# A recurrence's input products in four 64x64 tiles, with the side work listed by half steps

## The chip, the cores and the metric

The kernel runs on one core of a Trainium2 chip. Its metric is the time of one execution in device microseconds (us), from the first to the last instruction. The time before the change is the median of three runs. A profile of a single execution gives the rows that are read here.

The engines are called as the profile calls them: PE is the matrix engine (PEld is its weight load, which overlaps PE), ACT the scalar engine, DVE the vector engine, POOL the general-purpose engine, SP the queue that issues most transfers.

## The reference, cut to what matters

The whole is two transformer layers over 16 sequences of 512 tokens with 256 channels. The first layer (attention with latent heads, then a feed-forward part with weights and activations rounded to four bits) is not touched. The second layer begins with a recurrence over the 512 time steps, and only that part of the program changes:

```python
def _L1_attn_ref(tokens, norm_w, a, b, c, skip, w_out, b_out):
    B, T, DIM = tokens.shape
    H, D, S = b.shape                      # 16 heads, 16 channels each, 64 states each
    ms = jnp.mean(jnp.square(tokens), axis=-1, keepdims=True)
    x = tokens * jax.lax.rsqrt(ms + EPS) * norm_w
    x = x.reshape(B, T, H, D)
    a_t = jnp.tanh(a)
    state0 = jnp.zeros((B, H, S), dtype=tokens.dtype)

    def step(state, x_t):
        state = jnp.tanh(jnp.einsum('bhs,hst->bht', state, a_t) + jnp.einsum('bhd,hds->bhs', x_t, b))
        mixed = jnp.einsum('bhs,hsd->bhd', state, c) + skip[None] * x_t
        return (state, mixed)
    ...
    return tokens + outs @ w_out.T + b_out
```

After it come a layer norm, and a part without recurrence in time except that each token is mixed with the one before it: two products and a gate, then a third product, and a last layer norm.

A step's state depends on the state before it, so the 512 steps are a chain. The second term in the tanh, `x_t` times `b`, does not depend on the state: it is the input part of the title, and it can be computed for many steps at once.

## The kernel before

**Two groups.** The 16 heads are two groups `g` of 8, and a group's state of one step is a tile of 128 partitions (rows) by 64 columns. `advance_state(g, t)` (L1063) makes one step of one group: four matmuls (L1076) of state times `a`, added in PSUM to the input part that already stands there in the tile `u`, then two tanh instructions on ACT (L1084), which write the new state into `hist`. Each matmul of 32-bit floats is two instructions on PE, so the four are 8 PE instructions. The two groups alternate: while ACT works on one, PE works on the other. What stands between two calls of `advance_state` is called a half step below.

**Input part.** `inputs(u, g, t0, n)` (L1028) fills the tile `u` for up to 8 steps of one group. The weights `wb` have all 128 input rows and 64 columns, so two matmuls fit beside each other in the array (the profile writes 128*64 for that). For each step `u` has 64 columns, of which a half of the partitions uses one half of them, and the other half the other: 32 of 64 columns stay without an input part. A tile takes 16 matmuls with 64 columns each, cut into four pieces of four matmuls. `make_inputs(t)` (L1167) issues the pieces that are due at step `t`, right after the first group's step. In 16 steps that is 16 pieces.

**Side work.** All else of the second layer is worked on for blocks of 16 steps, some blocks ahead of or behind the recurrence, as generators that issue one piece at each call: N normalizes a block's tokens and turns them (two pieces, the second with four transposes on PE, L895, into the ring `xt`), R reads the states out (two pieces, L1052), A is the product with `w_out` (four, L916), M mixes neighbouring tokens (one, four transposes at L895), K and G are the products of key and gate (four each, L916), V is the last product (four, L916). The list `PERIOD` gives their order within 16 steps. At each step `left` says how many of the list's entries may be left over, so that the 21 entries are spread evenly: after the first group's step come the input piece and, where two entries fall on one step, the first of them; after the second group's step comes one entry. D is what is left of the first layer's feed-forward part of the last sequence (three times seven pieces); they stand in `LATER`, two thirds in the first 16 steps and one third in the next.

**Order.** PE's order is written out by hand: the matmuls stand in its queue in the order in which the Python code issues them. DVE, ACT and POOL are put in order by the scheduling layer, which places an instruction where it expects it to be ready. All engines work their queue strictly in order.

**States taken out.** After every 8 steps, four copies on POOL of one kind (L1208), four of another (L1212) and four copies on DVE (L1215) put the states from `hist` into the tile `clean`, in the layout that R reads. R of a block needs all copies of that block.

**Buffers.** PSUM has 8 banks: three tiles `u` of two banks each, and two banks for the results of all side work (`mm`, pool `ps_2`). A product that stays open from its first to its last piece holds one of these two banks until DVE or ACT has read it.

Of the kernel before, what the change touches and what calls it, by code (L numbers as in the profile page):

```python
# [59 lines left out]
def tile_kernel(ctx: ExitStack, tc: tile.TileContext, I: dict, out: bass.AP):  # L60
# [794 lines left out]
    def in_ring(g, t0):  # L855

        at = (t0 - g * 4) % RING
        cut = min(TS, RING - at)
        return [(0, at, cut)] + ([(cut, 0, TS - cut)] if cut < TS else [])
# [168 lines left out]
    def inputs(u, g, t0, n):  # L1028

        for k in range(2):  # L1030
            for par in range(2):
                at = (t0 - g * 4) % RING + par
                for half in range(2):
                    for r in range(2):
                        rs, bs = slice(r * 64, r * 64 + 64), half * 32 + r * 16
                        nc.tensor.matmul(  # L1036
                            u[rs, k, par:n:2, bs : bs + 16],
                            wb[:, g * 2 + k, par, half, rs], xt[:, g, at : at + n - par : 2, :],
                            start=par == 0 and half == 0, stop=False, skip_group_check=True,
                        )  # L1040
                yield
# [25 lines left out]
    def advance_state(g, t):  # L1067
        t0, _, u = us[g]
        if state[g] is not None:

            for k in range(2):
                own = state[g][:, k, :].rearrange("p (r s b) -> p r s b", r=2, s=2)
                into = u[:, k, t - t0, :].rearrange("p (s r b) -> p s r b", s=2, r=2)
                for c in range(2):
                    cs = slice(c * 64, c * 64 + 64)
                    nc.tensor.matmul(  # L1076
                        into[cs, :, c, :], ta[:, t % 2, g * 2 + k, cs], own[:, :, c, :],
# [3 lines left out]
        with tc.high_priority():  # L1081
            for r in range(2):
                rs = slice(r * 64, r * 64 + 64)
                nc.scalar.activation(  # L1084
                    state[g][rs, :, r * 32 : r * 32 + 32].rearrange("p k (s b) -> p k s b", s=2),
                    u[rs, :, t - t0, :]
                    .rearrange("p k (s r b) -> p k s r b", s=2, r=2)[:, :, :, r, :],
                    AF.Tanh,
                )

    def beside(M):

        todo = [("N", 1)] * 2 if M == 0 else []
        for e in PERIOD:
            i = M + int(e[1:])
            if 0 <= i < T // TS:
                todo.append((e[0], i))
        return todo + LATER.get(M, [])

    PERIOD = [
        "N2", "V-3", "V-3", "V-3", "V-3", "K-2", "K-2", "R-1", "R-1", "K-2", "K-2", "A-1", "A-1",
        "A-1", "A-1", "G-2", "G-2", "G-2", "G-2", "N2", "M-1",
    ]

# [5 lines left out]
    LATER = {  # L1112
        0: [
            *[("D", 1)] * 7, *[("D", 2)] * 7,
        ],
        1: [
            *[("D", 3)] * 7,
        ],
    }
# [3 lines left out]
        "U": lambda j: ffn_up(B - 1, j), "D": lambda j: ffn_down(B - 1, j),  # L1123
        "E": lambda j: iter([quantize_now(j) or 0.0]), "F": lambda j: iter([vector_done(("h", B - 1, j)) or 0.0]),
# [12 lines left out]
    with tc.manual_schedule(engines={mybir.EngineType.PE}):  # L1137
# [40 lines left out]
        for t in range(T):  # L1178
# [7 lines left out]
            if t == 0:  # L1186
                make_inputs(-1)
# [127 lines left out]
```

## Time and profile before

| what | us |
|---|---|
| median of three runs (2538.06 to 2540.24) | 2539.11 |
| span of the profiled execution | 2543.7 |
| in it: first layer, up to the first input product | 0 to 1814.0 |
| blocks 0 to 2 of 16 steps (first tanh of each: 1816.1, 1843.4, 1867.7) | 1816.1 to 1887.4 |
| blocks 3 to 30 | 1887.4 to 2491.6 |
| block 31, up to the last tanh | 2491.6 to 2514 |
| side work that is left after the last step | 2514 to 2543.7 |

Busy time over the whole span, from the first part of the page: PE 2412.0 us (95%), DVE 1925.8 us (76%), ACT 1621.3 us (64%), POOL 1035.4 us (41%). A busy share of PE is not PE at its peak, since matmuls are pipelined; what a step costs is read from the distance between the starts of instructions in the timeline.

The starts of the blocks are counted from the tanh instructions (L1084): 64 of them are one block of 16 steps of two groups. Blocks 3 to 30 take 604.25 us together, 21.58 us each on the mean, 1.35 us for a step. Block 0 takes 27.33 us, block 1 24.30, block 2 19.65 and block 31 20.12 us up to the start of what would be the next.

### The profile page before, as it was taken

How to read it: one execution, taken by the hardware profiler on the slowest of the kernel's cores; microseconds unless marked ns; L12 is line 12 of the kernel's file. 1: busy time of each engine (PE TensorE's matmuls, PEld its weight loads, DVE VectorE, ACT ScalarE, POOL GpSimd, SP SyncE). 2: the span in 40 equal slices, each digit the busy share in tenths (PEclk: the TensorE clock that was granted, in tenths of full speed). 3: DMA queues.
4: the chain of work that ended last, by engine and by line, in shares of the span. 5: the costliest groups of instructions: out<-in, count | busy, mean ns of one | idle time of the engine just before them, and what ended most of it. 6: DMA issues, size and time to landing. Idle time of an engine off the chain costs nothing.

```text
span 2543.7 us, 73791 instructions
## 1 busy us (share of the span) xinstructions
PE 2412.0 (95%) x28802; PEld 1712.7 (67%) x28802; DVE 1925.8 (76%) x5492; ACT 1621.3 (64%) x5536; POOL 1035.4 (41%) x1642
## 2 busy tenths in 40 slices
PE   7789999999999999999999999998799999999998
PEld 4455666666666666666666666655678888888885
DVE  4867888788888888888888888867756666666666
ACT  4656676676766666666666666654366666666664
POOL 4322333333333333333333333332445555555554
PEclk8889999999999999999999999989899999999999
DMA  3000000000000000000000000000111111111100
GB/s 117 24 9 6 12 24 14 16 16 12 24 14 16 16 12 24 14 16 16 12 24 14 16 14 6 16 14 9 43 32 39 37 40 41 40 38 39 36 28 27
DMA packets 58015, 61.30 MB, mean 24 GB/s; under 512 B 7873, under 2 KB 53058, under 8 KB 57666
## 3 DMA queue, kind: packets, MB, share of 16 engines
q1 hardware_dynamic: 56802, 55.54, 7.0%
q8 instruction: 226, 3.70, 0.6%
q14 instruction: 123, 1.01, 0.1%
q10 hardware_dynamic: 864, 1.05, 0.1%
HBM read 39.79 MB, written 16.78 MB: 22 GB/s over the span
## 4 chain that ended last, share of the span: by engine, by line
PE 51%; DVE 29%; ACT 10%; POOL 5%; issue 3%; DMA 1%; ACTq 0%; DVEq 0%; POOLq 0%; SPq 0%
PE u L1076 8%; DVE p L546 5%; PE ps_pt L569 5%; PE u L1036 5%; ACT p L559 4%; PE S L534 3%; PE ps_d L164 3%; DVE q_q L210 3%; ACT pT L571 3%; PE pg L164 3%; PE pu L164 2%; PE ps_h L449 2%; DVE q_sc L205 2%; DVE q_q L218 2%; PE ps_a L916 2%
## 5 line engine op out<-in xcount | busy, mean ns | idle before, releaser
L559 ACT ACTIVATE p<-p,nm 128x512 f32<-128x512 f32 (+3 forms) x1024 | 570.4, 562 | 492.3 <-DVE nm L546 488.3
L1084 ACT ACTIVATE hist<-u 64x64 f32<-64x64 f32 x2048 | 447.1, 218 | 237.4 <-PE u L1076 151.4
L546 DVE CUSTOM_DVE_ANT_0 p<-S,mask 128x512 f32<-128x512 f32 (+3 forms) x1024 | 442.9, 484 | 50.9 <-PE S L534 50.4
L1076 PEld LDWEIGHTS u<-hist,ta 128*64 128x64 f32 x8176 | 367.7, 138 | 119.9 <-ACT hist L1084 41.5
L569 PEld LDWEIGHTS ps_pt<-ident,p 128*128 128x128 f32 x2560 | 302.0, 142 | 217.3 <-issue 107.1
L571 ACT COPY pT<-ps_pt 128x384 f32<-128x384 f32 (+1 forms) x768 | 374.2, 517 | 62.3 <-PE ps_pt L569 62.1
L569 PE MATMUL ps_pt<-ident,p 128*128 128x128 f32 x2560 | 396.3, 280 | 4.5 <-DVE nm L546 3.0
L1076 PE MATMUL u<-hist,ta 128*64 128x32 f32 x8176 | 394.4, 218 | 4.6 <-ACT hist L1084 4.5
L219 POOL TENSOR_TENSOR q_q<-q_q,q_m 128x704 f32<-128x704 f32 (+1 forms) x140 | 164.1, 1172 | 372.2 <-DVE q_q L218 361.5
L534 PE MATMUL S<-kc,qr 32*128 32x512 f32 (+3 forms) x2048 | 224.1, 475 | 10.5 <-ACT qr L488 7.9
L1036 PE MATMUL u<-xt,wb 128*64 128x64 f32 x4128 | 224.9, 231 | 5.1 <-issue 5.0
L559 ACT ACTIVATION_READ_ACCUMULATOR p<-p,nm 128x1 f32 x1024 | 199.8, 195 | 0.0
L164 PE MATMUL ps_d<-wdT,hT 128*128 128x256 f32 x732 | 173.1, 386 | 13.9 <-DVE nm L546 12.1
L164 PE MATMUL pg<-wgT,xqT 128*128 128x352 f32 x512 | 177.9, 471 | 6.5 <-DVE nm L546 5.1
L483 POOL TENSOR_TENSOR qc<-qc,qs 128x512 f32<-128x512 f32 x64 | 81.5, 1273 | 235.5 <-DVE qs L482 221.1
L164 PE MATMUL pu<-wuT,xqT 128*128 128x352 f32 x512 | 173.7, 462 | 1.0 <-DVE nm L546 1.0
L1036 PEld LDWEIGHTS u<-xt,wb 128*64 128x64 f32 x4128 | 166.7, 140 | 10.3 <-issue 5.5
L600 PEld LDWEIGHTS py<-pT,vpad 128*32 128x32 f32 x5120 | 138.7, 110 | 47.0 <-issue 30.3
L600 PE MATMUL py<-pT,vpad 128*32 128x128 f32 x5120 | 162.6, 274 | 7.8 <-ACT pT L571 7.5
L164 PEld LDWEIGHTS ps_d<-wdT,hT 128*128 128x128 f32 x732 | 135.4, 192 | 37.6 <-DVE nm L546 15.4
L86 POOL TENSOR_SCALAR ve<-mv 128x2 f32<-128x2 f32 (+1 forms) x160 | 31.1, 194 | 312.4 <-DVE mv L94 309.7
L585 POOL COPY rcx<-rc 128x256 f32<-128x256 f32 x64 | 40.3, 630 | 286.9 <-DVE rc L583 260.9
(167 smaller groups left out, 4648.8 us busy)
## 6 DMA issues: line engine op xcount, KB each, us to landing
xT<-in_xT_dram SPq DMA_DIRECT2D x16, 512.0 KB
x<-in_x_dram SPq DMA_DIRECT2D x16, 512.0 KB
xs<-x SPq DMA_DIRECT2D x64, 128.0 KB
x<-xs SPq DMA_DIRECT2D x32, 256.0 KB
xm<-xs SPq DMA_DIRECT2D x32, 256.0 KB
out_dram<-o SPq DMA_DIRECT2D x64, 128.0 KB
w<-in_w_down_dram SPq DMA_DIRECT2D x2, 352.0 KB
w<-in_w_gate_dram SPq DMA_DIRECT2D x5, 128.0 KB
```

The costliest lines, as they stand in the source:

```text
L164: nc.tensor.matmul(dst, left, right, start=start, stop=stop)
L219: last.tensor_tensor(q, q, m, ALU.subtract)
L483: nc.gpsimd.tensor_tensor(of[k], of[k], x, ALU.add)
L534: nc.tensor.matmul(S[h][:, at : at + w], q[rs, i * P : i * P + P], k[rs, :w], start=True, stop=True,)
L546: nc.vector.tensor_tensor_reduce(out=p[:, own], in0=S[h][:, own], in1=mask[:, T - (i + 1) * P :], scale=1.0, scalar=-MASKED, op0=ALU.add, ...
L559: nc.scalar.activation(p[:, own], p[:, own], AF.Exp, bias=nm[:, u : u + 1], scale=-1.0, accum_out=sum_of[b, g][:, cb, half, h : h + 1],)
L569: nc.tensor.transpose(ps[:, at : at + P], p[:, at : at + P], ident)
L571: nc.scalar.copy(pT[:, :w], ps[:, :w])
L600: nc.tensor.matmul(py[q * 32 : q * 32 + 32, PLACE[i][1], :], vpad[b % 2][:, j, g * 4 + h, :], pt, start=j == 0 and h % 2 == 0, stop=j == i ...
L1036: nc.tensor.matmul(u[rs, k, par:n:2, bs : bs + 16], wb[:, g * 2 + k, par, half, rs], xt[:, g, at : at + n - par : 2, :], start=par == 0 an ...
L1076: nc.tensor.matmul(into[cs, :, c, :], ta[:, t % 2, g * 2 + k, cs], own[:, :, c, :], start=False, stop=True, skip_group_check=True,)
L1084: nc.scalar.activation(state[g][rs, :, r * 32 : r * 32 + 32].rearrange("p k (s b) -> p k s b", s=2), u[rs, :, t - t0, :] .rearrange("p k ( ...
```

## The change

`inputs` splits the 128 input rows in two halves `ks`. The weights are zero outside of the half that belongs to `k`, so each matmul now takes 64 rows and 64 columns, and the four combinations of `k` and `r` are four 64x64 tiles of the array. Four matmuls that follow each other are on four different tiles. The tile `u` has 32 columns for a step instead of 64, all of them used, so a tile of the same size holds 16 steps; one matmul has 128 columns (8 steps of 16 sequences). A tile takes 16 matmuls as before, now for 16 steps, in two pieces of eight matmuls. The matmuls of the recurrence write 32 columns that lie together instead of two times 16, and the two tanh instructions read them so; their number and size stay. The shift between the two groups' tiles is 8 steps instead of 4, also in the ring `xt` (`in_ring`).

The pieces are no longer spread by a count. `PERIOD` has 32 entries, one for each half step of a block, and each names what is issued behind that call of `advance_state`; many are empty. I and J are the input pieces of the two groups: both I pieces stand in one entry, the two J pieces in two. The D pieces fill the entries that are empty in the first blocks.

```diff
     def inputs(u, g, t0, n):

-        for k in range(2):
-            for par in range(2):
-                at = (t0 - g * 4) % RING + par
-                for half in range(2):
+        at = (t0 - g * 8) % RING
+        for par in range(2):
+            for half in range(2):
+                for k in range(2):
                     for r in range(2):
-                        rs, bs = slice(r * 64, r * 64 + 64), half * 32 + r * 16
+                        ks, rs = slice(k * 64, k * 64 + 64), slice(r * 64, r * 64 + 64)
                         nc.tensor.matmul(
-                            u[rs, k, par:n:2, bs : bs + 16],
-                            wb[:, g * 2 + k, par, half, rs], xt[:, g, at : at + n - par : 2, :],
+                            u[rs, k, par:n:2, half * B : half * B + B],
+                            wb[ks, g * 2 + k, par, half, rs], xt[ks, g, at + par : at + n : 2, :],
                             start=par == 0 and half == 0, stop=False, skip_group_check=True,
                         )
-                yield
+            yield 0.75
...
                     nc.tensor.matmul(
-                        into[cs, :, c, :], ta[:, t % 2, g * 2 + k, cs], own[:, :, c, :],
+                        u[cs, k, t - t0, :], ta[:, t % 2, g * 2 + k, cs], own[:, :, c, :],
                         start=False, stop=True, skip_group_check=True,
                     )
...
     def beside(M):

-        todo = [("N", 1)] * 2 if M == 0 else []
-        for e in PERIOD:
-            i = M + int(e[1:])
-            if 0 <= i < T // TS:
-                todo.append((e[0], i))
-        return todo + LATER.get(M, [])
+        todo = [[("N", 1)] * 2] if M == 0 else [[]]
+        for at, entry in enumerate(PERIOD):
+            now = todo[0] if at == 0 else []
+            for e in entry.split():
+                i = M + int(e[1:])
+                if e[0] in "IJ" and M < T // TS or 0 <= i < T // TS:
+                    now.append((e[0], i))
+            if not now and LATER:
+                now.append(LATER.pop(0))
+            if at:
+                todo.append(now)
+        return todo
...
     PERIOD = [
-        "N2", "V-3", "V-3", "V-3", "V-3", "K-2", "K-2", "R-1", "R-1", "K-2", "K-2", "A-1", "A-1",
-        "A-1", "A-1", "G-2", "G-2", "G-2", "G-2", "N2", "M-1",
+    PERIOD = ["V-3 V-3 N2", "", "J0", "", "R-1", "", "R-1", "", "J0", "A-1", "", "V-3", "V-3", "A-1", "", "K-2", "A-1", "A-1", "K-2", "", "K-2", "K-2", "", "I1 I1", "", "N2", "G-2", "G-2 G-2", "", "M-1", "", "G-2"
     ]
...
+        def next_inputs(g, t0):
+            if t0 >= T:
+                yield 0.0
+                yield 0.0
+                return
+            n = min(TS, T - t0) if t0 else TS - g * 8
+            u = ps_u.tile([P, 2, TS, 2 * B], F32, tag="u", name="u")
+            made[g, t0] = t0, n, u
+            yield from inputs(u, g, t0, n)
...
+            for g in range(2):
+                advance_state(g, t)
+                if g == 1 and t % 8 == 7:
+                    take_out(t)
+                for e in todo[t % TS * 2 + g]:
+                    step(*e)
```

The copies that take the states out are the same, in a function `take_out` of their own, and are issued at the same place. The first piece of N (its load, DVE and POOL work, no PE work) stands in the first entry of a block as before, its second at step 12 instead of 15; M stands at step 14 instead of 15. R stands at steps 2 and 3, where it was at step 6.

## The prediction

> **What bounds the kernel now.** I read first the page's groups of instructions, for the stage after 1814 us, where all changed lines run:
>
> ```profile
> L1084 ACT ACTIVATE hist<-u 64x64 f32<-64x64 f32 x2048 | 447.1, 218 | 237.4 <-PE u L1076 151.4
> L1076 PE MATMUL u<-hist,ta 128*64 128x32 f32 x8176 | 394.4, 218 | 4.6 <-ACT hist L1084 4.5
> L1036 PE MATMUL u<-xt,wb 128*64 128x64 f32 x4128 | 224.9, 231 | 5.1 <-issue 5.0
> ```
>
> ACT waits for the recurrence's matmuls, hardly ever the other way round: in this stage the path runs along PE's queue. Then the busy time of each engine in blocks 3 to 30:
>
> ```profile
> 1887.40:2491.60 604.20, 599.65 (x13180) 487.23 (x13179) 407.67 (x1067) 407.85 (x1840) 345.32 (x772) 1.00 0.13 38
> ```
>
> Of 604.20 us PE (second figure) is busy in 599.65, at the full granted clock (1.00); DVE, ACT and POOL are near 60% each. So what a block costs is the sum of PE's pieces, taken as distances between starts in PE's timeline:
>
> ```profile
> 2204.45 0.38 PE L1076 MATMUL u<-hist,ta 128*64 128x32 f32 x8
> 2204.66 0.43 PE L1036 MATMUL u<-xt,wb 128*64 128x64 f32 x8
> 2204.92 0.38 PE L1076 MATMUL u<-hist,ta 128*64 128x32 f32 x8
> 2205.12 0.63 PE L916 MATMUL ps_a<-woutT,ot 128*64 128x256 f32 x4
> 2205.59 0.37 PE L1076 MATMUL u<-hist,ta 128*64 128x32 f32 x8
> ...
> 2211.86 0.42 PE L1076 MATMUL u<-hist,ta 128*64 128x32 f32 x8
> 2212.22 0.66 PE L895 MATMUL ps_x<-ident,x 128*128 128x128 f32 x4
> 2212.81 0.43 PE L1076 MATMUL u<-hist,ta 128*64 128x32 f32 x8
> 2213.06 0.43 PE L1036 MATMUL u<-xt,wb 128*64 128x64 f32 x8
> 2213.32 0.38 PE L1076 MATMUL u<-hist,ta 128*64 128x32 f32 x8
> 2213.85 0.42 PE L1076 MATMUL u<-hist,ta 128*64 128x32 f32 x8 [0.15 <-ACT hist L1084]
> ...
> 2221.29 0.42 PE L1076 MATMUL u<-hist,ta 128*64 128x32 f32 x8
> 2221.65 0.64 PE L1052 MATMUL ro<-c,wc 128*32 128x256 f32 x8
> 2222.22 0.42 PE L1076 MATMUL u<-hist,ta 128*64 128x32 f32 x8
> ```
>
> A group's step is 0.21 us (0.25 with no product behind it), an input piece 0.26, a product piece (A, K, G, V) 0.465. R (0.57) and the transposes of N and M (0.59) come 0.36 instead of 0.21 us after the step ahead, since the tile shape changes (128*32, 128*128): 0.73 each with that gap. A step without side work has a floor: from 2212.81 to 2213.85, the same group again, 1.04 us by way of ACT.
>
> By this rule (a step costs its pieces, at least 1.04) the old order's 16 steps are: one without entry, 1.04; ten with one product, 0.21+0.26+0.21+0.465 = 1.145 each; three with two products, 1.61 each; one with R R and one with N M, 2.14 each. Sum 21.60; counted from the tanh instructions, a block takes 604.25/28 = 21.58. The rule holds for the old order, so I use it for the new.
>
> **The change, part by part.**
>
> Input pieces. Removed per block: 16 x 0.26 = 4.16 us of PE. Added: two J entries of 8 matmuls (16 PE instructions: four rounds of four tiles, 128 columns) and one I entry of twice that. No row shows 64*64. The stream: a product's 4 instructions are two rounds of 256 columns in 0.465 us, so four rounds of 128 take 0.465 if four tiles run at once. The loads: 8 of 64 columns fit into 0.205 (the step), 0.26 at most (the input piece), so 16 take 0.41 to 0.52. I take 0.48. Entry and exit come from the nearest row-split pair, two tiles of 64 rows:
>
> ```profile
> 1025.84 0.69 PE L467 MATMUL ps_q<-heads,bdq 64*128 64x512 f32 x1
> 1025.93 0.69 PE L467 MATMUL ps_k<-heads,bdk 64*128 64x512 f32 x1
> 1026.37 0.59 PE L467 MATMUL ps_q<-heads,bdq 64*128 64x512 f32 x1
> 1026.46 0.59 PE L467 MATMUL ps_k<-heads,bdk 64*128 64x512 f32 x1
> 1026.98 0.55 PE L569 MATMUL ps_pt<-ident,p 128*128 128x128 f32 x3
> ```
>
> ps_q and ps_k start 0.09 us apart and overlap, so row halves do run at once. The pair takes 1.14 us, of which two rounds of 512 columns are 0.93 (twice 0.465): 0.21 for getting in and out, and 0.15 for the gap ahead. J is 0.48+0.21+0.15 = 0.84, I I is 0.96+0.36 = 1.32; per block 2 x 0.84 + 1.32 = 3.00, that is 1.16 less than before. Bounds: 0.465 and 0.93 with only R's exit (0.57-0.465 = 0.105) and a gap of 0.11 give 0.68 and 1.145; if only two tiles run at once (the stream is then 0.93 and 1.86), 1.29 and 2.22.
>
> The Trainium skill's page "TensorE: Matmul & The Clock Gate", section "LDWEIGHTS (loading the stationary operand)", speaks against the change: a load takes its columns divided by 1.2 in ns, 53 ns for 64 columns. By that 16 loads would be an estimated 0.85 us, J 1.21 and I I 2.07, and a block 22.5 us, slower than now. The rows of the step do eight such loads with their matmuls in 0.21 us, 26 ns each, so I follow the rows.
>
> Places. In the new list (0.42 for the two groups, 0.46 with an empty half step) the steps are:
> 0: V V, 1.39. 1: J, 1.30. 2 and 3: R, 1.19 each. 4: J, A, 1.725. 5: V, 0.925, so 1.04. 6: V, A, 1.35. 7: K, 1.04. 8: A A, 1.35. 9: K, 1.04. 10: K K, 1.35. 11: I I, 1.78. 12: N, 1.19. 13: G, G G, 1.815. 14: M, 1.19. 15: G, 1.04.
> Sum 20.98, 0.62 less than 21.60. Of the 1.16 saved, 4 x 0.115 go to the floor of steps 5, 7, 9, 15 (the old order lost 0.32 to it in one step), the rest to more empty half steps. 28 blocks: -17.4 us.
>
> First blocks. Block 0 takes up all 21 D pieces. New: N, N 1.5; three D starts (6 transposes, 0.80 and the gap, from the rows of L333) 2.85; 18 D products 8.4; J J and I I 3.0; 30 half steps 6.3; steps 13 to 15 up to the floor 1.9; the slow clock at the start 1.8 (eight instructions take 0.45 us instead of 0.21 there); two waits of 0.6 for the copy hT, now only a half step ahead. Sum 26.9 against 27.33. Block 1 (no V, K, G, D): the list's sum less 0.35, 0.31, 0.31 and 0.775, 19.2, against 24.30. The old block 1 has a wait of 3.14 us where M's transposes stand right behind the layer norm of A; in the new list there are six steps between them, over 6 us, for a chain of some 4 us (L933 0.69, L93 0.75, L94 0.30, POOL's root 1.09, L903 0.74). Block 2 (no V): 20.3 against 19.65. Block 31 (no I, N): 20.1 against 20.12. Together -4.8.
>
> Edits at no cost. Writing 32 columns together and reading them so: the number and size of instructions stay, ACT's 218 ns too. take_out issues the same copies; they hide behind the next block's first steps as long as R finds them done, which is the second rival. The 1.1 us shorter distance from A's last product to V's output touches nothing on PE. No transfer is added; some on SP change places by one or two, and the only wait for a load in this stage is POOL's at L921, 1.6 us in all. After the last step the order of tasks up to the last store changes, but M of the last block still waits for A's layer norm: M starts 13.1 us after the last step now; the new order gives 13 (R behind copies at +3.7, then ot, four A): 0, within 1.
>
> Sum: -17.4 - 4.8 = -22.2. The profiled execution would go from 2543.7 to 2521.5. It lies 4.6 above the median of the runs; the difference holds for both: 2539.1 - 22.2 = 2516.9, say 2517. With the bounds on the cheap side (J 0.68, I I 1.145: 0.16 x 2 + 0.175, about 0.5 per block over 30 blocks) 2502; with 0.52 for the loads and 0.3 of new waits per block, 2530.
>
> **The rivals.**
>
> A. Four tiles run no better than two: the rounds of the two row halves follow each other. Against it: ps_q and ps_k above. For it: no row has both splits, and loads and stream are equally long here, so that each must hide the other. Price: J 1.29, I I 2.22, so 1.8 more per block, over 31 blocks +56: 2573. It decides once a J piece costs about 1.02 (0.18 more in each of four yields, 22 us); from there it is slower than before.
>
> B. A wait takes the saving's place: R, at step 2 instead of 6, waits for the copies of the last 8 states. Its second piece starts 1.39+1.30+1.19+0.36 = 4.24 us into the block. POOL needs 4 x 0.43 + 4 x 0.33 + 0.43 (carry) = 3.5 from the last tanh of the first group, DVE 0.68+0.69+1.74+1.40 = 4.5 from M's transposes, that is until 3.7. Margins of 0.5 to 0.7, if nothing stands in front; in the old trace an L921 of 1.28 lies between the copies. Late by 0.7 more than the margin in each of 31 blocks is +22: 2539. All engines behind PE would then wait with it, since the steps stand behind R in PE's queue.
>
> C. The floor by way of ACT leaves less than I think, because two tanh pairs that come close together push each other (0.47 each). It is in the floor as measured; 0.3 per block more gives 2526 and stays in the forecast's range.
>
> **How the numbers follow.** Forecast (C within it) 0.64, with its own range 2502 to 2530; A 0.17; B 0.19. A measurement tells 0.2%, 5 us, from no change. Faster: 0.64 and a third of B, less a little, 0.69; same: 0.12, B; slower: A and the rest of B, 0.19. The range goes from 2500 to 2556, which takes in B and the lower part of A, where four tiles overlap in part.
>
> **What would show it.** L1036 with 64*64 and half as many instructions; a J piece of 0.84 us from its first start to the next step, with the next group's step right behind; blocks of 21.0 us; no wait at L1052. A J piece of over 1.02 is A; idle time of PE ahead of L1052 put down to POOL or DVE copies is B. Wrong would be, too, a gain in blocks 3 to 30 that comes from other pieces than I and J, or none in block 1.

## The result, and the profile after

| | us |
|---|---|
| before, in the same session | 2539.68 |
| after, median of four runs (2556.30 to 2564.22) | 2560.93 |
| ratio | 1.0079, 95% interval 1.0063 to 1.0095 |
| profiled execution of after, span | 2561.7 (before: 2543.7) |

The change makes the kernel slower by 0.8%; 2517 was forecast, and the result lies 5 us above the range.

First a correction. The front part and the prediction counted tanh instructions in views that overlap at their edges, so that a few counted twice. Here a stretch begins at the start of the tanh that is exactly number 64 x M, and so for every kernel below. A block of before is then 21.65 us (21.58 there); the expectations quoted below still name the looser counts, 21.74 for after and 22.05 for tiles_alone, which are 21.85 and 22.08, and 27.6 and 26.9 for blocks 1 and 2 of after, which are 28.1 and 26.5. The first tanh itself is left out: it waits for no state, and it lies anywhere from 1804 to 1816 us though the first layer is unchanged. Single times are comparable to some 5 us only, so kernels are compared by stretches.

| stretch of the profiled execution | before | after | difference | forecast |
|---|---|---|---|---|
| start of block 1 | 1843.4 | 1840.3 | -3.2 | -0.4 |
| blocks 1 and 2 | 24.7 + 19.9 | 28.1 + 26.5 | +9.9 | -4.4 |
| blocks 3 to 30, each | 21.65 | 21.85 | +0.20, x 28 = +5.6 | -17.4 in all |
| block 31 | 19.4 | 19.2 | -0.3 | 0 |
| behind the start of the last tanh | 29.8 | 35.8 | +6.0 | 0 |

Together 18.0, the difference of the spans (differences are taken before rounding). So three stretches have to be explained. The groups of instructions of after that answer to those shown of before:

```profile
L1083 ACT ACTIVATE hist<-u 64x64 f32<-64x64 f32 x2048 | 447.2, 218 | 256.3 <-PE u L1075 185.7 <-PE u L1036 8.2 <-POOL c L1162 4.7
L1075 PE MATMUL u<-hist,ta 128*64 128x32 f32 x8176 | 379.0, 225 | 3.7 <-ACT hist L1083 2.5
```

ACT's idle time put down to PE has grown from 151.4 to 185.7 us while its own work is the same. And PE is no longer full; the busy times of the engines (PE, PEld, DVE, ACT, POOL, then PE's granted clock) in the window shown of before (in after it begins 7.5 us ahead of block 3):

```profile
1887.40:2491.60 604.20, 586.20 (x11288) 435.57 (x11282) 436.28 (x1053) 404.33 (x1823) 356.11 (x765) 1.00 0.13 37
```

586.20 us instead of 599.65 with x11288 instructions instead of x13180: the saving of PE is there, and 18 us of the window are now idle. PE's timeline shows both, the cheap input pieces and a wait:

```profile
2201.67 0.61 PE L1075 MATMUL u<-hist,ta 128*64 128x32 f32 x16
2202.21 0.67 PE L1036 MATMUL u<-xt,wb 64*64 64x128 f32 x16
2202.81 0.77 PE L1075 MATMUL u<-hist,ta 128*64 128x32 f32 x16
2204.14 0.98 PE L1052 MATMUL ro<-c,wc 128*32 128x256 f32 x8 [0.56 <-POOL c L1166]
2205.05 0.66 PE L1075 MATMUL u<-hist,ta 128*64 128x32 f32 x16
2205.64 0.89 PE L1052 MATMUL ro<-c,wc 128*32 128x256 f32 x8
2206.46 0.66 PE L1075 MATMUL u<-hist,ta 128*64 128x32 f32 x16
...
2216.39 1.10 PE L1036 MATMUL u<-xt,wb 64*64 64x128 f32 x32
2217.43 0.66 PE L1075 MATMUL u<-hist,ta 128*64 128x32 f32 x16
```

L1036 is 64*64 with 16 instructions, and the next step starts 0.60 us after it. Ahead of it the two groups' steps (x16) take 0.54 where the forecast's sum has 0.46 for such a pair, so in its terms J costs 0.68 us; two I pieces (x32) take 1.04, and 1.12 with the same 0.08 ahead. R (L1052) waits 0.56 us for POOL's copy into `c`, and its two pieces then take 0.91 and 0.82 from start to start instead of 0.57, because in each of them later instructions wait for later copies. POOL's own timeline in that stretch:

```profile
2195.49 1.04 POOL L971 TENSOR_TENSOR ka<-ka 128x512 f32<-128x512 f32 x1
2196.57 1.28 POOL L921 TENSOR_TENSOR xm<-xm,bout 128x512 f32<-128x512 f32 x1
2199.55 0.19 POOL L875 TENSOR_SCALAR ss<-ss 128x2 f32<-128x2 f32 x1 [1.71 <-DVE ss L871]
2199.83 0.74 POOL L877 TENSOR_TENSOR rs<-ss,neg_half 128x2 f32<-128x2 f32 x1
2200.68 1.38 POOL L879 TENSOR_SCALAR xn<-x,rs 128x256 f32<-128x256 f32 x2
2202.01 1.65 POOL L1162 COPY c<-hist 64x256 f32<-64x256 f32 x3
2203.61 1.17 POOL L1166 COPY c<-hist 64x128 f32<-64x128 f32 x3
2204.82 0.40 POOL L1162 COPY c<-hist 64x256 f32<-64x256 f32 x1
```

The copies (L1162, L1166) start at 2202.01, behind N's three instructions (L875, L877, L879), and these had waited 1.71 us for DVE (L871). The scheduling layer has put N ahead of the copies, and POOL keeps its queue's order.

### The profile page after: what moved, and what is told of

It is laid out like the page before. It is cut to its first block, busy times and chain, and to the rows that moved or that the text cites. A ratio compares the mean times of both kernels' runs of the same rounds, so it can differ in the third digit from the quotient of the medians.

```text
span 2561.7 us, 69750 instructions
## 1 busy us (share of the span) xinstructions
PE 2412.2 (94%) x26754; PEld 1667.7 (65%) x26754; DVE 1958.8 (76%) x5492; ACT 1621.2 (63%) x5536; POOL 1050.0 (41%) x1642
## 3 DMA queue, kind: packets, MB, share of 16 engines
q10 hardware_dynamic: 864, 1.05, 0.1%
## 4 chain that ended last, share of the span: by engine, by line
PE 40%; DVE 38%; ACT 9%; POOL 7%; issue 4%; DMA 0%; POOLq 0%; DVEq 0%; ACTq 0%; SPq 0%
PE u L1075 5%; DVE p L546 5%; PE ps_pt L569 5%; ACT p L559 4%; PE S L534 3%; PE ps_d L164 3%; DVE q_q L210 3%; ACT pT L571 3%; PE ps_h L449 3%; PE pg L164 2%; DVE q_q L218 2%; DVE q_sc L205 2%; DVE bnst L93 2%; PE pu L164 2%; DVE x L903 2%
## 5 line engine op out<-in xcount | busy, mean ns | idle before, releaser
L1083 ACT ACTIVATE hist<-u 64x64 f32<-64x64 f32 x2048 | 447.2, 218 | 256.3 <-PE u L1075 185.7
L1075 PEld LDWEIGHTS u<-hist,ta 128*64 128x64 f32 x8176 | 344.8, 141 | 150.2 <-ACT hist L1083 77.3
L1075 PE MATMUL u<-hist,ta 128*64 128x32 f32 x8176 | 379.0, 225 | 3.7 <-ACT hist L1083 2.5
L1162 POOL COPY c<-hist 64x256 f32<-64x256 f32 x256 | 121.0, 473 | 158.8 <-ACT hist L1083 147.9
L164 PE MATMUL ps_d<-wdT,hT 128*128 128x256 f32 x732 | 172.6, 385 | 14.2 <-DVE nm L546 12.4
L585 POOL COPY rcx<-rc 128x256 f32<-128x256 f32 x64 | 40.2, 629 | 288.4 <-DVE rc L583 269.4
L534 PEld LDWEIGHTS S<-kc,qr 32*128 32x128 f32 x2048 | 104.6, 185 | 71.4 <-issue 31.7
L310 DVE SCALAR_TENSOR_TENSOR th<-th,pg 128x352 f32<-128x352 f32 x128 | 66.2, 517 | 94.1 <-ACT th L309 94.1
```

The lines of the kernel that those rows point to most:

```text
L164: nc.tensor.matmul(dst, left, right, start=start, stop=stop)
L534: nc.tensor.matmul(S[h][:, at : at + w], q[rs, i * P : i * P + P], k[rs, :w], start=True, stop=True,)
L1075: nc.tensor.matmul(u[cs, k, t - t0, :], ta[:, t % 2, g * 2 + k, cs], own[:, :, c, :], start=False, stop=True, skip_group_check=True,)
L1083: nc.scalar.activation(state[g][rs, :, r * 32 : r * 32 + 32], u[rs, :, t - t0, :], AF.Tanh,)
L1162: nc.gpsimd.tensor_copy(new[rs, at : at + 8 : 2].rearrange("p t k s b -> p t k (s b)"), old[rs, 0::2, :, r].rearrange("p t k s b -> p t k ...
```

## The experiments

Unless it is said otherwise a kernel is the changed one with the edit shown. The table has every run's stretches, read in the same way; "ratio" is against the kernel before in the same session, where it was timed in rounds.

| kernel | us (runs) | ratio, 95% interval | block 1 begins | blocks 1+2 | blocks 3 to 30, each | behind the last tanh |
|---|---|---|---|---|---|---|
| before | 2539.68 (4) | 1 | 1843.4 | 44.7 | 21.65 | 29.8 |
| after | 2560.93 (4) | 1.0063 to 1.0095 | 1840.3 | 54.6 | 21.85 | 35.8 |
| tiles_alone | 2558.05 (4) | 1.0037 to 1.0074 | 1843.3 | 49.5 | 22.08 | 29.8 |
| half_tanh | 2506.29 (1) | | 1841.8 | 44.5 | 20.42 | 29.8 |
| no_norm_pool | 2537.66 (1) | | 1841.5 | 54.7 | 20.91 | 34.9 |
| copies_first | 2568.47 (1) | | 1844.6 | 46.3 | 22.20 | 35.1 |
| pool_order | 2530.00 (1) | | 1837.3 | 55.5 | 20.74 | 35.5 |
| before_pool | 2543.73 (1) | | 1838.7 | 42.3 | 21.64 | 35.8 |
| d_spread | 2562.34 (4) | 1.0064 to 1.0094 | 1842.4 | 50.7 | 21.84 | 35.7 |
| warm | 2551.60 (1) | | 1843.8 | 40.2 | 21.81 | 35.5 |
| old_tail | 2563.61 (1) | | 1846.0 | 54.7 | 21.85 | 29.7 |
| even | 2552.17 (4) | 1.0028 to 1.0058 | 1842.5 | 52.5 | 21.48 | 32.9 |
| even_warm_tail | 2545.87 (10) | 1.0010 to 1.0029 | 1844.9 | 42.5 | 21.52 | 36.1 |
| best | 2520.59 (1) | | 1840.6 | 43.5 | 20.77 | 32.7 |
| best_pool | 2522.51 (4) | 0.9903 to 0.9936 | 1845.7 | 40.4 | 20.74 | 36.0 |
| three_mended | 2517.98 (4) | 0.9895 to 0.9928 | 1845.4 | 40.5 | 20.76 | 34.1 |
| pool_steps | 2513.87 (4) | 0.9884 to 0.9919 | 1840.8 | 40.4 | 20.74 | 29.9 |

### The tiles without the list, and ACT's share

**tiles_alone** is the kernel before with the changed `inputs` and `advance_state` (64*64 products, tiles of 16 steps) and the old list:

```diff
-            [(t0, 8) for t0 in range(0, T, 8)],
+            [(t0, 16) for t0 in range(0, T, 16)],
...
-                for q in range(4):
-                    pieces.append((t0 - 4 + q, g, t0, n))
+                for q in range(2):
+                    pieces.append((t0 - 7 + q * 3 if g else t0 - 5 + q, g, t0, n))
```

> The kernel before with the four 64x64 tiles and 16-step tiles alone; its own list and count of pieces stay. If the tiles are cheap as in the changed kernel's trace (16 instructions in 0.60 us plus 0.04 ahead, so 4 x 0.64 = 2.56 us per block against 4.16), the step rule gives 21.35 us per block against 21.60: the 1.6 us saved on PE mostly falls to the floor of 1.04 us in ten steps that are left with one product. So 2530 to 2536 us, a little faster than before. Rival: the tile shape change is what costs, through steps that it breaks up; then blocks of over 22 us and 2550 or more.

2558.05: a miss, and the rival's number: it seems to speak against the tiles themselves. No wait at R here, and yet a block takes 22.08 us. PE's and ACT's timelines:

```profile
2202.22 0.66 PE L1075 MATMUL u<-hist,ta 128*64 128x32 f32 x16
2203.27 0.42 PE L1075 MATMUL u<-hist,ta 128*64 128x32 f32 x8 [0.39 <-ACT hist L1083]
2203.62 0.67 PE L1036 MATMUL u<-xt,wb 64*64 64x128 f32 x16
```

```profile
2202.76 1.49 ACT L1083 ACTIVATE hist<-u 64x64 f32<-64x64 f32 x6 [0.72 <-PE u L1075]
```

Without an input piece between them the two groups' steps stand back to back (x16). Their tanh pairs queue on ACT: six instructions in 1.49 us, 0.50 us for a pair. The next step starts 1.05 us later, 0.39 of it idle, and whatever stands behind that step waits too. To test this, **half_tanh** is tiles_alone with one tanh of two left out, so that half of each state stays at its first value:

```diff
-            for r in range(2):
+            for r in range(1):
                 rs = slice(r * 64, r * 64 + 64)
                 nc.scalar.activation(
```

> As tiles_alone, but of the two tanh instructions of each step of a group only the first is done; the other half of each state is left at its first value, so the recurrence is computed on half of its states only. PE's instructions are the same ones in the same order. Theory 'tanh chain': in tiles_alone the PE time saved fell into ACT's chain, where a tanh pair behind another one takes 0.52 us (2202.76: six in 1.49; 2212.58: ten in 2.59) and two groups without a piece between them queue there; with 0.26 per group instead, the chain by hand gives 20.3 us per block instead of 22.05, so 2558 - 28 x 1.75 = about 2509, and the waits of PE for hist all but gone. Rival 'the tiles cost PE more than their rows show' (changing between 64*64 and 128*64 slows the steps beside them): blocks stay at 21.7 to 22, time 2548 or more.

20.42 us per block, and 2506.29: a hit, with every PE instruction as in tiles_alone. The weight loads' idle time in blocks 3 to about 30 (last figures: idle, and its releasers):

```profile
L1075 PEld LDWEIGHTS u<-hist,ta 128*64 128x64 f32 x6744 | 285.8, 137 | 150.8 <-ACT hist L1083 98.0 <-issue 4.7
```

```profile
L1075 PEld LDWEIGHTS u<-hist,ta 128*64 128x64 f32 x7330 | 309.6, 137 | 123.0 <-ACT hist L1083 51.3 <-issue 5.5
```

98.0 us put down to `hist` fall to 51.3. So in tiles_alone at least 1.66 us of a block are ACT's chain, and the saving of PE had fallen into it. The floor of 1.04 us that the forecast knew is part of these 1.66: a step with one product takes 0.90 in half_tanh (2202.35 to 2203.25). In before the same row shows 35.6 us put down to `hist`, so the old order hid more of the chain; that the input piece between the groups is what hid it is read from the order and not tried by itself.

The rival holds for a small part. PE's timeline of half_tanh around an input piece:

```profile
2205.48 0.37 PE L1075 MATMUL u<-hist,ta 128*64 128x32 f32 x8
2205.78 0.67 PE L1036 MATMUL u<-xt,wb 64*64 64x128 f32 x16
2206.38 0.42 PE L1075 MATMUL u<-hist,ta 128*64 128x32 f32 x8
2206.63 0.63 PE L916 MATMUL ps_a<-woutT,ot 128*64 128x256 f32 x4
```

The step ahead of the piece takes 0.30 us and the one behind it 0.25, where the old input piece (128*64, as the steps) leaves 0.21 and 0.20. So the piece costs 0.14 us beside its own 0.60, not the 0.04 of the expectation. With four pieces in a block that is an estimated 0.4 of the 0.73 us by which 22.08 exceeds the expected 21.35; the other 0.3 is left for what ACT's chain adds to the floor.

### What holds R

**no_norm_pool** leaves out N's work on POOL, so that something else than the normalized tokens goes into the ring:

```diff
-        nc.gpsimd.tensor_scalar(ss, ss, 1.0 / C, RMS_EPS, ALU.mult, ALU.add)
-        rs = small.tile([P, 2], F32, tag="rs", name="rs")
-        nc.gpsimd.tensor_tensor(rs, ss, neg_half[:, :2], ALU.pow)
-        for i in range(2):
-            nc.gpsimd.tensor_scalar(xn[:, i, :], x[:, i, :], rs[:, i : i + 1], 1.0, ALU.mult, ALU.mult)
```

> The changed kernel without N's three kinds of work on POOL (the root and the scaling of the tokens are left out, so the tokens are not normalized). Theory (POOL held): the copies that R waits for start 1.5 us into a block because N's work stands ahead of them on POOL; without it they start with the last tanh, PE's wait at R goes, blocks 3 to 30 fall from 21.74 to about 20.7 us, the whole by 25 to 30 us to some 2533. Rival: the copies are too long by themselves for R at step 2; then the wait at R stays over 0.3 us in each block and the gain is under 15.

**copies_first** gives the copies priority with the scheduler:

```diff
-                    take_out(t)
+                    with tc.high_priority():
+                        take_out(t)
```

> The changed kernel with the copies out of hist issued at high priority. That puts DVE's four copies ahead of M's work on DVE, while POOL's still stand behind N's. Theory (POOL held): the first product of R waits as before for POOL's copies, at most its second gets shorter; within 8 us of 2561. Rival: DVE's copies are the late ones; then 15 us or more are gained.

Without N's work 20.91 us per block, and no wait at R. With priority 22.20: DVE's copies moved ahead of most of M's work, POOL's stayed behind N's. R still waits for POOL (0.20 us, and its first piece takes 0.99), its second piece is back at 0.57, and a new wait of 0.87 us for DVE's `xt` stands ahead of M's transposes. So POOL's copies hold R, and priority does not move them. Whether it is the work left out or the order stays open with these two. **pool_order** leaves nothing out and keeps POOL's queue as the program lists it (the filling of the next `x3T` from `carry`, which the scheduler had placed early, is moved to where the carry is made):

```diff
+        with tc.manual_schedule(engines={mybir.EngineType.PE, mybir.EngineType.Pool}):
             for t in range(T):
...
-        xT = wk2.tile([P, 2, B + 2 * P], F32, tag="x3T", name="x3T")
-        nc.gpsimd.tensor_copy(xT[:, :, :B], carry)
+        xT = x3T_next.pop()
         nc.vector.tensor_copy(xT[:, :, B:], ps)
         nc.gpsimd.tensor_copy(carry, xT[:, :, 2 * P :])
+        turned_next()
```

> As after, all work done and the list unchanged; only POOL's queue in this stage is kept in the order in which the program lists it (the copies of the last 8 states, then N's three instructions), and the copy of carry into the next x3T stands right behind the copy of x3T into carry. Theory 'POOL held': R's wait for the copies shrinks from about 1.5 us per block to 0.3 to 0.8, blocks 3 to 30 go from 21.74 to 21.0 to 21.4, 2541 to 2551 in all. Rival 'the copies are late by themselves or for DVE's share': L1052 waits as long as in after, 21.6 to 21.8 per block, 2558 or more.

20.74 us per block, better than expected, and 2530.00, below the kernel before. POOL's and PE's timelines around R:

```profile
2206.60 0.40 POOL L1170 COPY c<-hist 64x256 f32<-64x256 f32 x1
2206.94 0.29 POOL L1174 COPY c<-hist 64x128 f32<-64x128 f32 x1
2207.32 0.19 POOL L875 TENSOR_SCALAR ss<-ss 128x2 f32<-128x2 f32 x1
```

```profile
2205.45 0.79 PE L1082 MATMUL u<-hist,ta 128*64 128x32 f32 x16
2206.18 0.64 PE L1059 MATMUL ro<-c,wc 128*32 128x256 f32 x8
2206.74 0.66 PE L1082 MATMUL u<-hist,ta 128*64 128x32 f32 x16
2207.33 0.64 PE L1059 MATMUL ro<-c,wc 128*32 128x256 f32 x8
2207.90 0.80 PE L1082 MATMUL u<-hist,ta 128*64 128x32 f32 x16
```

N's L875 now comes behind the last copy (L1174), and R (L1059 here) has no idle time ahead of it and its old 0.57 us from start to start. From the step behind J to the step behind R the PE takes 2.45 us where after took 3.65. The control is the same edit on the kernel before:

> The kernel before, with POOL's queue in the program's order as in pool_order and nothing else. Theory 'PE's sum bounds the old order, POOL's order matters only since the change': blocks 3 to 30 stay at 21.6 to 21.8 us (21.65), 2535 to 2546 in all, so that pool_order's 20.74 is the change's own gain set free. Rival 'POOL's order is worth an us per block in any kernel': 20.9 or less, 2523 or less.

21.64 us per block, as without it. The edit orders all of POOL's queue and not N alone; that N is what stands ahead of the copies is shown by no_norm_pool (20.91). The order of POOL is worth nothing in the kernel before; the 0.91 us per block of pool_order are the change's own saving, set free.

### Blocks 1 and 2

The new list puts all 21 D pieces into block 0; its last three steps and many half steps of blocks 1 and 2 are left empty. **d_spread** lets a block take seven of them at most:

```diff
-            if not now and LATER:
+            if not now and LATER and len(LATER) > 21 - 7 * (M + 1):
```

> The changed kernel with at most seven D pieces in a block, so that they fill blocks 0 to 2 instead of block 0 alone. Theory (clock): blocks 1 and 2 of the changed kernel take 27.6 and 26.9 us because PE has too little to do there and is granted a low clock (0.70 in that window); with D they keep the clock and take 20 to 22 us each, block 0 some 21: the whole 2544 to 2550 us. Rival: they are long because of the waits at R and between steps, then nothing changes, 2556 to 2564.

A miss: 2562.34, the rival's number. The slow stretch moved and split: block 0 now has empty half steps of its own, the clock is granted at 0.50 from 1829.5 to 1850.0 and again from 1867.1 to 1873.9, and blocks 1 and 2 take 50.7 us. So this run does not decide between theory and rival. **warm** instead fills steps that have no entry at all with one product whose result is never read. The edit makes ten of them, not the nine that the expectation counts: three at the end of block 0, six in block 1 and one in block 2.

```diff
+    def keep_warm(j):
+        ps = mm("ps_w")
+        by_64(ps[:, : 2 * P], sq["wkT"][:, 0, :P], sq["wvT"][:, 0, :], True, True)
+        yield 0.46
...
+            elif not now and M < 3 and at % 2 and not todo[at - 1]:
+                now.append(("W", M * 32 + at))
```

> As after, with one product of no use (four instructions, 0.465 us, its result is never read) in each step of blocks 1 and 2 that has no entry in either half: seven in block 1, two in block 2. They lie under the 1.04 us that such a step takes by way of ACT. Theory 'clock': these blocks run at a granted clock of 0.50 because PE has too little to do (windows of 6 us with about 100 PE instructions lose the clock, those with 116 and more hold it); with the products the clock stays nearer 1.00, blocks 1 and 2 fall from 27.62 and 26.89 to 20 to 23 each: about 2548. Rival 'the steps there are slow for another reason, the clock only follows': no gain, 2561 or a little more.

19.5 and 20.7 us: a hit, though the single time is 3 us above the expected one. Windows in block 1 of after and of warm (the granted clock is the third figure from the end):

```profile
1842.00:1860.00 18.00, 17.34 (x228) 12.82 (x220) 3.90 (x13) 8.47 (x39) 5.47 (x14) 0.50 0.12 31
```

```profile
1842.00:1860.00 18.00, 17.69 (x370) 13.32 (x368) 8.04 (x25) 12.92 (x60) 9.90 (x23) 1.00 0.13 40
```

228 PE instructions in 18 us at a clock of 0.50, and 370 at 1.00. The rows of after in that window are the same instructions as in block 17 above (2205.05 to 2206.46, R without its wait 0.57), each at half speed:

```profile
1842.41 1.07 PE L1075 MATMUL u<-hist,ta 128*64 128x32 f32 x16
1843.41 1.08 PE L1052 MATMUL ro<-c,wc 128*32 128x256 f32 x8
1844.42 1.07 PE L1075 MATMUL u<-hist,ta 128*64 128x32 f32 x16
```

More work for PE made it finish the same steps 14.4 us sooner. In after the clock is at 0.50 from 1840.1 to 1884.5, near the end of block 2, but for 3.4 us at 1864. It falls at the end of block 0, where steps stand alone:

```profile
1837.76 3.66 PE L1075 MATMUL u<-hist,ta 128*64 128x32 f32 x56 [0.33 <-ACT hist L1083]
```

Seven steps of a group follow each other with no product between, which is where warm has its first three. PE stands idle for at most 0.33 us there, so it is not a long wait that loses the clock.

### Behind the last step

**old_tail** lists the remaining pieces in the order that the old list gave them:

```diff
-        for M in range(T // 16, T // 16 + 4):
-            for now in beside(M):
-                for e in now:
-                    step(*e)
+        for e in "V3 K2 R1 A1 G2 M1 V2 K1 G1 V1".split():
+            for _ in range({"M": 1, "R": 2}.get(e[0], 4)):
+                step(e[0], T // TS - int(e[1:]))
```

> As after, but the pieces behind the last step in the order that the old list gave them: V29, K30, R31, A31, G30, M31, V30, K31, G31, V31, each with all its pieces; nothing else. Theory 'order of the tail': in after V29's and A31's pieces are cut up by the list, M31 stands behind K30 and G30 and starts 15 us after the last step; with the old order the stretch from the last tanh to the end goes from 35.8 back to about 30 us, 2555 in all. Rival 'the tail is slow because PE's clock falls there': 34 us or more, 2559 or more.

29.7 us instead of 35.8, a hit; the single time is no lower because that execution reached block 1 5.8 us later. PE's timeline behind the last step of after, and of old_tail:

```profile
2526.94 0.86 PE L1052 MATMUL ro<-c,wc 128*32 128x256 f32 x8 [0.15 <-POOL c L1166]
2529.03 0.89 PE L1052 MATMUL ro<-c,wc 128*32 128x256 f32 x8 [1.24 <-DVE c L1169]
2530.99 0.65 PE L916 MATMUL ps_a<-woutT,ot 128*64 128x256 f32 x4 [1.06 <-DVE ot L1061]
...
2540.94 1.09 PE L895 MATMUL ps_x<-ident,x 128*128 128x128 f32 x4 [3.48 <-DVE x L903]
2542.91 3.68 PE L916 MATMUL ps_kv<-wvT,ka 128*64 128x256 f32 x16
```

```profile
2535.76 1.07 PE L1052 MATMUL ro<-c,wc 128*32 128x256 f32 x16 [0.53 <-DVE th L1002]
2538.10 1.97 PE L916 MATMUL ps_a<-woutT,ot 128*64 128x256 f32 x16 [1.27 <-DVE ot L1061]
...
2543.46 0.67 PE L895 MATMUL ps_x<-ident,x 128*128 128x128 f32 x4 [1.66 <-DVE x L903]
2544.06 1.95 PE L916 MATMUL ps_kv<-wvT,ka 128*64 128x256 f32 x16
```

M's transposes (L895) start 15.0 us after the last tanh of after (2525.9) and 11.8 us after that of old_tail (2531.7); in before it is 12.3. In after R's second piece waits for a copy on DVE, A comes in parts between V and K, and M waits 3.48 us for A's layer norm. In that wait the clock falls again: V30's 16 instructions take 3.68 us instead of 1.95, 1.7 of the 6.0 us.

### Other lists, and all three together

**even** changes the list alone: R in steps 5 and 7, M in the next block, long pieces and pairs of products by turns. **even_warm_tail** adds warm's products and a tail that begins with M30. **best** moves M to the front, V to steps 2 and 3, R to 4 and 5, and has M30, R31, V29, A31, K30, G30, M31, V30, K31, G31, V31 behind the last step; **best_pool** adds POOL's listed order. Their lists:

```diff
 even, even_warm_tail
+        "V-3", "V-3", "J0", "", "M-2", "", "V-3", "V-3", "J0", "", "R-1", "", "K-2 N2", "K-2", "R-1", "",
+        "K-2", "K-2", "I1", "", "A-1", "A-1", "I1", "", "A-1", "A-1", "N2", "", "G-2", "G-2", "G-2", "G-2",
 best, best_pool
+        "M-2", "", "J0", "", "V-3", "V-3", "V-3", "V-3", "R-1", "", "R-1", "", "K-2 N2", "K-2", "J0", "",
+        "K-2", "K-2", "I1", "", "A-1", "A-1", "A-1", "A-1", "I1", "", "N2", "", "G-2", "G-2", "G-2", "G-2",
```

> As after, with another list alone: R's two pieces in steps 5 and 7 instead of 2 and 3, M in step 2 of the next block, the norm of N's tokens started in step 6, and the entries laid so that a step has either one long piece (J, I, R, N, M) or two products and no half step of one is empty in both halves. Theory 'POOL held, and tanh chain': R finds its copies done, no wait at L1052; by hand with ACT's chain 20.5 to 20.9 us per block 3 to 30 instead of 21.74, so 24 to 34 less: 2527 to 2537, with blocks 0 to 2 and the tail as slow as in after. Rival 'the saving is lost in PE itself, whatever the order': 21.4 or more per block, 2551 or more.

> The list of even, the products of no use of warm, and after the last step the order M30, V29, R31, A31, K30, G30, V30, M31, K31, G31, V31, each with all its pieces. If the theories 'POOL held, and tanh chain' and 'clock' hold, and the tail goes back from 35.8 to about 30 us: blocks 3 to 30 at 20.5 to 20.9, blocks 0 to 2 at 65 to 70 instead of 79.7, together 2507 to 2523, faster than the kernel before. If only the list helps: 2524 to 2537. If neither: 2545 or more.

> The kernel even_warm_tail with one more list and tail: M in half step 0 of the next block, V in 4 to 7, R in 8 and 10, K in 12, 13, 16, 17, A in 20 to 23, I in 18 and 24, N in 26, G in 28 to 31; behind the last step M30, R31, V29, A31, K30, G30, M31, V30, K31, G31, V31. POOL's queue as the scheduler makes it: N's three instructions may stand between the copies. Theory 'A waited for ot because DVE's queue stood behind V's layer norm, whose factor POOL computes behind the copies' (0.66 us per block in even): with V three half steps earlier and R as early as the copies allow, no wait at A; if POOL's N does not hold R, 20.5 to 20.9 per block and about 2525; if it does, a wait at L1052 of 0.3 to 0.8 and about 2535 to 2540. Rival 'the list cannot take more out': 21.3 or more, 2541 or more.

> The kernel best with POOL's queue kept in the program's order as in pool_order. Theory as there: neither R nor A waits, 20.4 to 20.8 us per block 3 to 30, blocks 0 to 2 at 70 to 73, the stretch behind the last tanh 28 to 31: 2517 to 2530, faster than the kernel before. Rival: waits go on to another place (K for the mixed tokens of M, V for th): 21.2 or more, 2537 or more.

even: a miss, and by its number (21.48, 2552.17) the rival's case; best's 20.77 below shows that the order does count. R waits no more, but 21.48 is above the 20.5 to 20.9 expected, since a new wait stands at A. PE's and DVE's timelines:

```profile
2209.42 0.65 PE L916 MATMUL ps_a<-woutT,ot 128*64 128x256 f32 x4 [0.66 <-DVE ot L1061]
```

```profile
2206.43 0.48 DVE L1061 SCALAR_TENSOR_TENSOR ot<-xt,cols,ro 128x256 f32<-128x256 f32 x1
2208.11 0.74 DVE L903 TENSOR_SCALAR o<-x,mv,rstd 128x256 f32<-128x256 f32 x2 [1.21 <-POOL rstd L88]
2208.76 0.60 DVE L1061 SCALAR_TENSOR_TENSOR ot<-xt,cols,ro 128x128 f32<-128x128 f32 x2
```

The first part of `ot` (L1061) is ready at 2206.9; then DVE stands 1.21 us before V's layer norm (L903), for a factor that POOL computes behind its copies, and the rest of `ot` comes behind that. With V and R moved away from each other best has 20.77 and no such wait, also without POOL's listed order: the list can solve what the queue's order solves. Neither list goes below the change's own list with POOL in order (20.74), so evenness of the steps brought nothing here. even_warm_tail, with 2545.87, ended in the last of its three cases: warm's products hold (42.5 us in blocks 1 and 2), the list has even's wait, and its tail takes 36.1 us. best and best_pool met their figures for blocks 3 to 30; best_pool's tail missed (36.0).

**three_mended** is the change with its own list and the edits of pool_order, warm and old_tail. **pool_steps** is the same, with POOL's listed order only up to the last step:

> The change with its own list, and the three edits of pool_order, warm and old_tail together: POOL's queue as listed, products of no use in the empty steps of blocks 1 and 2, the old order behind the last step. If the three causes add up: blocks 3 to 30 at 20.7 to 20.8 us (21.85 in after), blocks 1 and 2 at about 20 each instead of 28.1 and 26.5, 29.7 behind the last tanh instead of 35.8; 31 + 14 + 6 = 51 less than after's 2561: 2506 to 2514. If they share a cause, or one gives back what another gains: 2520 or more.

> As three_mended, but POOL's queue is kept as listed only up to the last step; behind it the scheduler orders POOL again. In three_mended the stretch behind the last tanh is 34.1 us instead of old_tail's 29.7, and there L903 of V29 takes 2.40 us for its two instructions beside POOL's L983 and L921, ahead of A31's layer norm. Theory 'the listed order of POOL costs 4 us behind the last step': 29.5 to 31 there, 2512 to 2516 in all. Rival 'the old order of pieces is slower there since the change, whatever POOL does': 33 or more, 2517 to 2520.5.

three_mended has 20.76 per block and 40.5 us in blocks 1 and 2 as expected, but 34.1 us behind the last tanh, so 2517.98 is a near miss. before_pool shows the same from the other side: its tail went from 29.8 to 35.8 with POOL's order alone. pool_steps brings 29.9 back: 2513.87, 1.0% faster than the kernel before (0.9884 to 0.9919), and the best of those that do all the work. Against after its span is 50.6 us shorter: 31.1 in blocks 3 to 30, 14.2 in blocks 1 and 2, 5.9 behind the last tanh, less 0.6 because block 1 begins later. The three causes add up.

## Why the prediction was wrong, step by step

**Input pieces: the mechanism right, the size too large.** J was put at 0.84 us and I I at 1.32; they are 0.68 and 1.12 with the gap, the cheap end of the bounds (0.68 and 1.145). Rival A is refuted: four tiles do run at once. The 53 ns for a load of 64 columns, an estimate from the Trainium skill's page "TensorE: Matmul & The Clock Gate", section "LDWEIGHTS (loading the stationary operand)", do not show: 16 loads with their matmuls take 0.60 us, at most 38 ns each.

**The sum of the new list, 20.98, was right for a POOL queue that the change did not have.** With POOL in order a block takes 20.74. Two errors cancel in that: the input pieces are cheaper by some 0.5 per block (2 x 0.16 + 0.20), and the rule "a step costs its pieces, at least 1.04" leaves out some 0.3. That the two meet so nearly is luck.

**Rival C had about the right size and was left out of the sum.** "0.3 per block more" was said to be in the floor as measured, and put at nothing. The floor came from one step by itself; the steps around it also queue their tanh pairs on ACT. What the rule leaves out in the new list, some 0.3, is of C's size; that it is the chain is shown for tiles_alone (by half_tanh), not for the new list.

**Rival B came true: the wait at R, which the sum put at nothing, was the largest error.** It had a chance of 0.19 and a price of 0.7 per block. Its words were "Margins of 0.5 to 0.7, if nothing stands in front". Something does: N's three instructions on POOL, which end 1.5 us after the block's start (2202.0, the block starting at 2200.5). The order of POOL's queue was taken over from the old trace, where N's L875 to L879 come behind the copies; the sentence "take_out issues the same copies" looked at what is issued and not at where it lands in a queue that the scheduler orders. The price fits: R's wait is 1.1 us per block (21.85 less 20.74), 31 us in all. With the cheaper pieces (-0.5) and the 0.3 that the rule leaves out it makes the forecast -0.62 per block into about +0.2, and -17.4 into +5.6.

**Blocks 1 and 2: 19.2 and 20.3 forecast, 28.1 and 26.5 measured.** The sum priced every instruction at full clock. The slow clock at the start was seen and priced (1.8 us), but not that a stretch with little to do loses it again. In before block 1 had seven D pieces and both had 16 input pieces, and the clock was 0.96 on the mean of the two; after has 0.63 there. warm gives 14.4 us back and takes 19.5 and 20.7, close to the forecast, so the cause is shown.

**Behind the last step: "0, within 1", measured +6.0.** "M of the last block still waits for A's layer norm" was right, but the 13 us were worked out with R at +3.7 and four A pieces in a row. The list puts V pieces between A's, and DVE's copies stand behind M30's work, so that M starts at 15.0; old_tail gives 5.9 to 6.1 back.

Forecast and best version nearly meet, 2517 and 2513.87, but that is no merit of the forecast: it needs three edits that it did not foresee.

## What to carry to other kernels

Moving a step in a hand-written order moves it against queues that are ordered by somebody else: build the new kernel, read the order of each such queue around the moved step, and price the wait with that order, not with the old trace's. A piece of work that is removed may have been the spacer that hid another chain, so price a step's floor with its neighbours and not alone. And price a stretch with little PE work at the lower clock: here 41 us at 0.50 cost 14.4 us.

## What the runs showed of the hardware

**PE's clock.** Read in windows of 6 us, after loses it in the two windows in which PE's instructions fall from 120 to 98 and 88 (granted clock 1.00, 0.84, 0.50), and has 0.50 to 0.66 for the next 36 us, with 72 to 89 instructions each (fewer also because they run slower); three_mended, with 106 to 132 there, keeps 1.00. PE still counts as busy for 17.34 of 18 us in the slow stretch: a full busy column beside a clock of 0.50 is light work, slowed down. It is no matter of the count alone, since some windows of block 0 with 90 and 92 instructions, D's longer ones among them, kept 1.00; so the border that warm's expectation names, about 100 to 116, is none. Where one lies was not tried.

**DVE beside POOL.** The same instruction takes three times as long while POOL works beside it. DVE's L903 (128x256 in place, with two factors) in blocks 3 to about 30 (minimum, median, maximum in ns):

```profile
L903 DVE TENSOR_SCALAR x<-x,mv,rstd x53: 406/411/417, 1906.3 to 2469.7; 128x256 f32<-128x256 f32 x53
```

```profile
L903 DVE TENSOR_SCALAR x<-x,mv,rstd x52: 1112/1238/1392, 1910.1 to 2460.6; 128x256 f32<-128x256 f32 x52
L903 DVE TENSOR_SCALAR o<-x,mv,rstd x52: 405/410/416, 1907.4 to 2457.2; 128x256 f32<-128x256 f32 x52
```

411 ns become 1238 for A's (`x`), where POOL runs L971 and L921 at the same time (2195.49 to 2197.85, DVE's L903 from 2195.56 for 2.43 us), and stay 410 for V's (`o`), where it does not. It is 759 in pool_order and 450 in best. That DVE's delay here is what pushes N's L871, and with it L875, into the copies' way is read from the timeline and not tried by itself; and which of POOL's two instructions does it was not tried either.
